# Two attention layers on one core: where the softmax division stands, and how the row maximum is formed

## The chip, the cores and the metric

The kernel runs on one core of a Trainium2 chip, as one program. The metric is the device time of one execution in microseconds (us); of the kernel before three executions were timed, with a median of 2111.77 us (2107.32 to 2115.55).

## The reference, cut to what matters

The input x has the shape (2, 512, 512): 2 batches, 512 tokens, width 512, all fp32. Four blocks follow each other, each as `x = x + LN(block(LN(x)))`:

```
L0 attention: 32 query heads, 8 key/value heads of 128, rotary, causal
    attn = softmax(q k^T / sqrt(128) with mask);  out = (attn v) Wo^T
L0 feed-forward: one linear layer with low-rank terms
L1 attention: 32 heads of 128, biases, rmsnorm on q and k, no mask
    attn = softmax(q k^T / sqrt(128));            out = (attn v + bv) Wo + bo
L1 feed-forward: silu(x w1) * (x w3), then w2, each with low-rank terms
```

The softmax of a row is exp(s - max) divided by the sum of the row. The change is about this division, and in layer 1 about the maximum and the factor 1/rms of q (`rq`), which is a factor of a row of the scores.

## The kernel before, in words

All products are made exact to fp32 by splitting each operand into a high and a low part of type fp32r (`hi + lo = x`) and adding three matmuls, hi hi + hi lo + lo hi (`mm3`). So every operand costs a cast to `hi` (ScalarE or VectorE) and a subtraction for `lo` (GpSimd or VectorE) before TensorE may use it.

A unit is two heads of one batch; there are 32 units in each attention layer, 64 heads a layer. For each head and each tile of 128 queries (`qt`, four of them):

- `l0_score` or `l1_score`: the scores in a PSUM bank (`ps_s`). In layer 0 one VectorE instruction adds the mask and takes the maximum. In layer 1 VectorE reduces the bank to the maximum (`m`), and a second, one element wide, multiplies it by `rq` (`mr`).
- `softmax_tail`: ScalarE makes P = exp(scale s + bias) from the bank, with the sum of the row (`rs`); VectorE takes the reciprocal (`ri`, one column); `nc.mul` multiplies the tile of P by it, on whichever of GpSimd, VectorE and ScalarE is done first by the program's own estimates. The page names this tile `ar`, as all large tiles.
- In most units (`lag`: units 2 to 26 of layer 0 and, counting on, 33 to 62, so 55 units or 110 heads) P is then transposed as 32 x 32 blocks on VectorE, written to DRAM (`pc` in layer 0, `pd` in layer 1), and read back with the blocks in place. Two tiles of queries make one such read of four DMAs. Casts and subtractions give `hi` and `lo` of P^T.
- `av_items`: O^T = V^T P^T in a PSUM bank (`ps_oy`), about one head later. ScalarE casts it to `hi`, VectorE subtracts for `lo` (the two `ot` tiles), in layer 1 with the bias `bv`.
- `out_proj`: y += O Wo, four matmul groups a unit.

In the other units (`pv_items`) P is transposed on TensorE at once.

The order of every engine's instructions is fixed when the program is built. A planner in the same file keeps a clock for TensorE and for each engine, with costs of its own; an item of TensorE's work is issued when its condition (`ok`) holds on that clock, and each stage of the other engines' work is issued at the time at which the planner expects its input. All DMAs are issued by SyncE, in one queue, in the planned order. The large tiles come from an arena of 37 slots of 4 KB a partition, each of which holds one full or two half tiles; `NBUF` and `PHASES` bound how many of each kind may live.

Of the kernel before, what the change touches and what calls it, by code (L numbers as in the profile page):

```python
# [19 lines left out]
S = 512  # L20
D = 512
P = 128
# [34 lines left out]
class Item:  # L57
    """a piece of TensorE's work, to be issued when cond holds"""
# [5 lines left out]
class Engine:  # L64
    """An engine that keeps its order of issue, with a clock (us) of its work."""
# [58 lines left out]
class Engines:  # L124
    WEIGHT = dict(vector=1.0, scalar=0.5, gpsimd=0.0)

    def pick(self, *cands):
        """issue the one of the candidates (engine, op, args...) that is done first"""
        def score(x):
            e = getattr(self, x[0])  # L130
            kw = x[-1] if isinstance(x[-1], dict) else {}
            c = e.cost(x[1], [y for y in x[2:] if not isinstance(y, dict)], kw)
            t = max(e.free, e.k.now + LAT)
            for y in x[2:]:
                if isinstance(y, bass.AP) and y.space == PSUM:
                    t = max(t, e.k.banks.get(y.name, 0.0))
            return t + c * (1 + self.WEIGHT[x[0]])
        x = min(cands, key=score)
        kw = x[-1] if isinstance(x[-1], dict) else {}
        return getattr(getattr(self, x[0]), x[1])(*[y for y in x[2:] if not isinstance(y, dict)], **kw)  # L140
# [9 lines left out]
    def mul(self, out, a, s):  # L150
        """by a factor of each row"""
        self.pick(("gpsimd", "tensor_scalar", out, a, s, 1.0, ALU.mult, ALU.mult),
                  ("vector", "tensor_scalar", out, a, s, None, ALU.mult),
                  ("scalar", "activation", out, a, AF.Copy, dict(scale=s)))

    def copy(self, out, a):
        """from PSUM"""
        self.pick(("scalar", "copy", out, a), ("vector", "tensor_copy", out, a))
# [8 lines left out]
class Kern:  # L167
    """Work is written as items: functions, or generators that yield the time
    (of TensorE's work) after which their next stage is to be issued."""

    NBUF = dict(TN=1, KT=2, W=14, Wk=4, raw=3, bb=2, bqk=1, nat=2, qk=10, v=4, P=7, x=8, xn=2, pt=5, T=4, PT=3, ot=6, tmp=2, A=5,
                v32=2, q32=4, k32=3, p32=1,
# [44 lines left out]
    # the large tiles: a half or the whole of a slot each (halves of one type only in a slot)  # L217
    HALF = dict(W=2, Wk=1, nat=2, v=2, PT=2, TN=2, KT=2, raw=1, bb=1, bqk=1, qk=1, P=1, x=1, A=1, T=1, xn=1, pt=1, ot=1,
# [77 lines left out]
    def phase(self, i):  # L296
        """what is tuned for each phase of the work"""
        for k, v in PHASES[i].items():
            if k in self.NBUF:
                self.NBUF[k] = v  # L300
            elif k in self.nc.WEIGHT:
                self.nc.WEIGHT[k] = v
            else:
                setattr(self, k, v)
# [20 lines left out]
    def wait(self, tag, n=1):  # L325
        """in a stage: until n slots are free, first come first served"""
        q = self.queues.setdefault(tag, [])
        ticket = object()
        q.append(ticket)
        while q[0] is not ticket or not self.has(tag, n):  # L330
            yield 0.1
        q.pop(0)

    def low(self, eng):
        """in a stage of low priority: until the engine has nothing issued to it"""
        e = getattr(self.nc, eng)
        while e.free > self.now + 0.01:
            yield e.free - self.now
# [6 lines left out]
    def streams(self, main, fills, bg):  # L345
        """Issue the streams of items, each in its order: a fill when its nominal place in
        main has come, or main waits; bg starts at its nominal place."""
# [30 lines left out]
    def pe(self, t):  # L378
        """t: at the full clock, which TensorE has after a busy tick only"""
        s = max(self.clk, self.now)  # L380
        while s >= self.tick:
            self.warm = self.cols >= 3060
            self.cols = 0
            self.tick += 10.24 / 3
        self.cols += t * 2400
        self.clk = self.now = s + (t if self.warm else 2 * t)
# [6 lines left out]
    def mm3(self, out, pairs, start=True, stop=True):  # L393
        """exact hi/lo products: hi hi + hi lo + lo hi"""
        n = len(pairs)
        for i, (lh, ll, rh, rl) in enumerate(pairs):
            self.mm(out, lh, rh, start and i == 0, False)
            self.mm(out, lh, rl, False, False)
            self.mm(out, ll, rh, False, stop and i == n - 1)
# [6 lines left out]
    def setup(self):  # L406
# [11 lines left out]
        self.pd = [self.dr.tile([P, 2, 4, 256], F32, name=f"pd{i}") for i in range(3)]  # L418
        self.kd = {n: [self.dr.tile([P, 4, 256], F32, name=f"kd{n}{i}") for i in range(2)] for n in "kq"}
# [9 lines left out]
    def consts(self):  # L429
# [5 lines left out]
        nc.vector.scalar_tensor_tensor(self.g, self.gqk[:, 0:1], SCALE, self.gqk[:, 1:2], ALU.mult, ALU.mult)  # L435
# [6 lines left out]
    def split(self, hi, lo, raw):  # L442
        """hi + lo = raw exactly"""
# [105 lines left out]
    def resid(self, b, tt, lvl):  # L549
        """x of level lvl + 1 = x + LN(y); returned short of a constant of each row"""  # L550
# [10 lines left out]
        if lvl == 3:  # L561
# [10 lines left out]
            nc.sync.dma_start(self.xsrc(b, tt, 4), x)  # L572
            self.rel(x)
# [6 lines left out]
        def store():  # L580
# [8 lines left out]
            nc.sync.dma_start(self.xsrc(b, tt, lvl + 1), xo)  # L589
            self.rel(xo)  # L590
# [3 lines left out]
    def boundary(self, b, tt, lvl):  # L594
        """from the finished y of level lvl on"""
# [21 lines left out]
    def out_proj(self, b, first, last, ot, w, badd, lvl):  # L617
        """y += O Wo over the heads of this unit"""
# [62 lines left out]
    def softmax_tail(self, st, j, qt, ps, bias, scale, w):  # L681
# [3 lines left out]
        rs = self.t("rs", [P, 1])  # L685
        nc.scalar.activation(pr[:, :w], ps[:, :w], AF.Exp, bias=bias, scale=scale, accum_out=rs)
        yield
        self.rel(bias, ps)
        ri = self.t("ri", [P, 1])
        nc.vector.reciprocal(ri, rs)  # L690
        yield
        nc.mul(pr[:, :w], pr[:, :w], ri)
        yield
        self.rel(rs, ri)
        if not st.get("lag"):
            st["p", j, qt] = pr
            return
        # P^T = 32 x 32 blocks transposed on VectorE, and the blocks put in place on their way through DRAM
# [60 lines left out]

    def unit_done(self, st):  # L760
        """after the last use of V"""
# [5 lines left out]
    def pv_items(self, st, j, voff, causal, bias):  # L767
        """transposes of P, then O^T = V^T P^T, split"""
# [70 lines left out]
    def av_items(self, st, j, voff, bias):  # L839
        """O^T = V^T P^T by halves of the queries, split"""  # L840
# [4 lines left out]
        def av(h, kc):  # L845
# [17 lines left out]
            if j == 1:  # L863
                self.unit_done(st)
            oh = self.t("ot", [P, S], F32R)
            ol = self.t("ot", [P, S], F32R)
            if bias is None:
                nc.scalar.copy(oh, po)
                yield
                nc.vector.tensor_tensor(ol, po, oh.bitcast(F32), ALU.subtract)  # L870
            else:
                nc.scalar.activation(oh, po, AF.Identity, bias=bias)
                yield
                nc.vector.scalar_tensor_tensor(ol, po, bias, oh.bitcast(F32), ALU.add, ALU.subtract)
            yield
            self.rel(po)
            st["ot"].append((oh, ol))

        def ok(h, kc):
            return (("hl", j, h, kc) in st and "v" in st["v"] and ((h, kc) != todo[0] or self.free("ps_oy"))  # L880
                    and ((h, kc) != todo[-1] or self.free("ot", 2)))
        return [Item(lambda h=h, kc=kc: ok(h, kc), lambda h=h, kc=kc: av(h, kc), 0, True) for h, kc in todo]

# [13 lines left out]
    def l0_zero(self):  # L897
        """the parts of pd0 that stay unused"""
# [135 lines left out]
    def l1_pre(self, hp, b, w, lag):  # L1034
# [62 lines left out]
        def flip(n):  # L1097
            """the transposes as 32 x 32 blocks on VectorE, put in place on their way through DRAM"""
# [70 lines left out]
    def l1_score(self, st, j):  # L1169
        def one(qt):  # L1170
# [6 lines left out]
            m = self.t("m", [P, 1])  # L1177
            nc.vector.tensor_reduce(m, ps, AX.X, ALU.max, negate=True)
            yield
# [3 lines left out]
            mr = self.t("mr", [P, 1])  # L1183
            nc.vector.tensor_tensor(mr, m, r, ALU.mult)
            yield
            self.rel(m)
            yield from self.softmax_tail(st, j, qt, ps, mr, r, S)
# [47 lines left out]
    def f1_init(self):  # L1235
        """rows 0:16, 32:48, 64:80 of the pieces: hi of a low-rank factor, lo in block k; others 0"""
# [151 lines left out]
    def f1_post(self, js, b, sts, last):  # L1388
        """y += g W2 over the chunks of units js"""
# [32 lines left out]
    def run(self, nu0=16, nu1=16, nf=6):  # L1422
        # at the ends of a layer's units some run batch by batch, each then with weights of its own
# [18 lines left out]
        def pre(n):  # L1442
            """early, mid items and state of unit n"""
# [47 lines left out]
        # weights start this many units before (early, mid, late parts)  # L1491
# [144 lines left out]
def _layout(i):  # L1636
    """Layouts of the arrays only: transposes and tilings."""
# [45 lines left out]
```

## Time and profile before

| what | value |
| --- | --- |
| median of three executions | 2111.77 us |
| lowest, highest | 2107.32, 2115.55 us |
| the profiled execution: its span | 2117.8 us |
| mean granted TensorE clock in it | 0.993 |
| instructions | 41211 |
| DMA traffic in it | 370.54 MB, mean 175 GB/s |
| ScalarE busy | 1337.7 us (63%) |
| GpSimd busy | 1446.3 us (68%) |

The page gives no other time for the profiled execution than its span; this span is 6.0 us (0.3%) over the median. A row of the page is read as: engine, operation, output<-inputs by tile names, shape, count; then busy time in all, mean time of one in ns, and the idle time of the engine in front of it with the instruction that ended it. Nearly all instructions have one line of code, since a helper issues them, so rows are told apart by tiles and shapes. The stages can be told by time: layer 0 attention runs to about 700 us, its feed-forward to about 770, layer 1 attention to about 1900, and the layer 1 feed-forward to the end.

### The profile page before, as it was taken

How to read it: one execution, taken by the hardware profiler on the slowest of the kernel's cores; microseconds unless marked ns; L12 is line 12 of the kernel's file. 1: busy time of each engine (PE TensorE's matmuls, PEld its weight loads, DVE VectorE, ACT ScalarE, POOL GpSimd, SP SyncE). 2: the span in 40 equal slices, each digit the busy share in tenths (PEclk: the TensorE clock that was granted, in tenths of full speed). 3: DMA queues.
4: the chain of work that ended last, by engine and by line, in shares of the span. 5: the costliest groups of instructions: out<-in, count | busy, mean ns of one | idle time of the engine just before them, and what ended most of it. 6: DMA issues, size and time to landing. Idle time of an engine off the chain costs nothing.

```text
span 2117.8 us, 41211 instructions
## 1 busy us (share of the span) xinstructions
PE 2056.7 (97%) x12605; PEld 1827.5 (86%) x12605; DVE 1801.4 (85%) x4210; ACT 1337.7 (63%) x3247; POOL 1446.3 (68%) x1786
## 2 busy tenths in 40 slices
PE   8999999999999999999999999999999999989998
PEld 7888888888888798889899999999999898977886
DVE  7998899899888889889889999899989988888534
ACT  5776677577766668776666666666667666664212
POOL 5686678688875567877677777777777776774212
PEclk9999999999999999999999999999999999999999
DMA  2476567577652235887877777777777787763021
GB/s 98 127 183 166 145 185 183 143 200 199 177 159 66 71 103 166 244 232 223 227 202 229 220 227 211 207 221 219 225 206 232 213 240 212 224 178 93 31 67 44
DMA packets 476566, 370.54 MB, mean 175 GB/s; under 512 B 117400, under 2 KB 424488, under 8 KB 476344
## 3 DMA queue, kind: packets, MB, share of 16 engines
q1 hardware_dynamic: 476344, 367.91, 60.9%
q8 instruction: 99, 1.62, 0.3%
q14 instruction: 123, 1.01, 0.2%
HBM read 232.12 MB, written 135.66 MB: 174 GB/s over the span
## 4 chain that ended last, share of the span: by engine, by line
PE 54%; DMA 12%; DVE 9%; SPq 3%; issue 2%; POOL 2%; ACT 2%; DVEq 0%; ACTq 0%; POOLq 0%
PE ps_pj L102 23%; PE ps_oy L102 19%; PE ps_s L102 10%; DVE ar L102 6%; SPq L102 3%; DMA pd<-ar 3%; DMA ar<-pd 2%; POOL ar L102 2%; DMA kdk<-ar 2%; ACT ar L102 2%; DMA ar<-kdq 2%; DMA kdq<-ar 2%; PE ps_tr L102 1%; DMA ar<-pc 1%; DVE m L102 1%
## 5 line engine op out<-in xcount | busy, mean ns | idle before, releaser
L102 POOL TENSOR_TENSOR ar<-ar,ar 128x256 fp32r<-128x256 f32 (+4 forms) x1223 | 1058.3, 887 | 456.6 <-ACT ar L102 333.6
L102 PE MATMUL ps_oy<-ar,ar 128*128 128x256 f32 (+2 forms) x4014 | 832.2, 342 | 28.7 <-DVE ar L102 14.0
L102 PEld LDWEIGHTS ps_oy<-ar,ar 128*128 128x128 f32 x4014 | 653.5, 190 | 133.1 <-DVE ar L102 22.5
L102 ACT CAST ar<-ar 128x256 fp32r<-128x256 f32 (+3 forms) x1166 | 531.5, 490 | 305.4 <-DMA ar<-pd 117.1
L102 PE MATMUL ps_pj<-ar,xh 128*128 128x256 f32 (+1 forms) x3392 | 635.2, 285 | 0.9 <-POOL ar L102 0.6
L102 PEld LDWEIGHTS ps_pj<-ar,xh 128*128 128x128 f32 x3392 | 536.0, 190 | 14.5 <-POOL ar L102 1.1
L102 PE MATMUL ps_pj<-ar,xl 128*128 128x256 f32 (+1 forms) x1696 | 482.9, 285 | 0.0
L102 DVE STREAM_TRANSPOSE ar<-ar 128x256 f32<-128x256 f32 (+3 forms) x688 | 347.9, 533 | 16.9 <-DMA pd<-ar 9.7
L102 DVE TENSOR_TENSOR ar<-ps_pj,ar 128x512 f32<-128x512 f32 (+2 forms) x448 | 305.4, 683 | 52.5 <-PE ps_pj L102 44.8
L102 PE MATMUL ps_s<-ar,ar 128*128 128x512 f32 (+2 forms) x1252 | 338.5, 376 | 8.6 <-DVE ar L102 4.7
L102 PEld LDWEIGHTS ps_pj<-ar,xl 128*128 128x128 f32 x1696 | 322.9, 190 | 2.1 <-DVE xl L102 0.7
L102 PE MATMUL ps_pj<-xh,ar 128*128 128x512 f32 x816 | 286.6, 399 | 0.7 <-ACT xh L102 0.7
L102 DVE TENSOR_TENSOR y<-ps_oy,y 128x512 f32<-128x512 f32 x272 | 184.8, 680 | 81.8 <-PE ps_oy L102 80.2
L102 PEld LDWEIGHTS ps_s<-ar,ar 128*128 128x128 f32 x1252 | 214.5, 189 | 44.0 <-DVE ar L102 12.6
L102 DVE TENSOR_TENSOR ar<-ar,ar 128x256 fp32r<-128x256 f32 (+5 forms) x328 | 207.9, 652 | 51.1 <-ACT ar L102 50.1
L102 ACT ACTIVATE ar<-ps_s,mr,rq 128x512 f32<-128x512 f32 x256 | 198.6, 777 | 46.7 <-DVE mr L102 36.9
L102 PEld LDWEIGHTS ps_pj<-xh,ar 128*128 128x128 f32 x816 | 154.0, 189 | 31.7 <-ACT xh L102 1.1
L102 DVE TENSOR_REDUCE m<-ps_s 128x1 f32<-128x512 f32 x256 | 170.9, 673 | 6.2 <-PE ps_s L102 5.0
L102 ACT ACTIVATE ar<-ar,ri 128x512 f32<-128x512 f32 (+3 forms) x245 | 149.6, 621 | 38.3 <-DVE ri L102 37.1
L102 POOL TENSOR_SCALAR ar<-ar,ri 128x512 f32<-128x512 f32 (+3 forms) x202 | 133.0, 661 | 54.3 <-DVE ri L102 48.9
L102 PE MATMUL ps_pj<-xl,ar 128*128 128x512 f32 (+1 forms) x408 | 161.2, 395 | 0.0
L102 ACT ACTIVATE ar<-ps_s,m 128x512 f32<-128x512 f32 (+3 forms) x256 | 133.8, 526 | 23.4 <-DVE m L102 14.8
(91 smaller groups left out, 2105.5 us busy)
## 6 DMA issues: line engine op xcount, KB each, us to landing
pd<-ar SPq DMA_DIRECT2D x240, 256.0 KB, 3.7
ar<-pd SPq DMA_DIRECT2D x480, 128.0 KB, 3.3
ar<-pc SPq DMA_DIRECT2D x200, 128.0 KB, 3.0
ar<-in_wq SPq DMA_DIRECT2D x86, 256.0 KB, 4.1
ar<-in_wo SPq DMA_DIRECT2D x86, 256.0 KB, 3.6
kdk<-ar SPq DMA_DIRECT2D x31, 512.0 KB, 4.8
ar<-kdk SPq DMA_DIRECT2D x124, 128.0 KB, 4.0
kdq<-ar SPq DMA_DIRECT2D x31, 512.0 KB, 5.1
```

The lines of the kernel that those rows point to most:

```text
L102: r = self.k.tc.keep_in_program_order(f(*args, **kw))
```

## The change

In the 55 units with `lag` P is no longer divided. The sums of a head's four tiles go into one tile `rs4` of four columns; when the fourth is there, `row_factors` takes one reciprocal of all four, writes it to DRAM (`rd`, 128 rows of 16 bytes) and reads it back into a half slot `R`, the same 512 values in all 128 partitions. When O^T is complete, one VectorE instruction multiplies the PSUM bank by R into a new half slot `ob`, with R read at a step of four elements; the casts and subtractions for `ot` then read `ob`, and the layer 0 subtraction may go to GpSimd. The last group of an O^T is planned only when R is planned to be there. In layer 1, in all units, one VectorE instruction multiplies the scores in place by `rq` and takes the minimum in the same pass; the sign is turned (`-SCALE`), so the minimum is minus the maximum, and the exponential has the constant scale -1. In two places the planner keeps a tile until its store has landed. The comments are taken out, which changes no instruction. The core of the diff:

```diff
     NBUF = dict(...
-                v32=2, q32=4, k32=3, p32=1,
+                R=2, ob=1, rs4=3, ri4=2, v32=2, q32=4, k32=3, p32=1,
...
+        self.rd = [self.dr.tile([P, NT], F32, name=f"rd{i}") for i in range(3)]
...
-        nc.vector.scalar_tensor_tensor(self.g, self.gqk[:, 0:1], SCALE, self.gqk[:, 1:2], ALU.mult, ALU.mult)
+        nc.vector.scalar_tensor_tensor(self.g, self.gqk[:, 0:1], -SCALE, self.gqk[:, 1:2], ALU.mult, ALU.mult)
...
             nc.sync.dma_start(self.xsrc(b, tt, lvl + 1), xo)
+            yield
             self.rel(xo)
...
-        rs = self.t("rs", [P, 1])
-        nc.scalar.activation(pr[:, :w], ps[:, :w], AF.Exp, bias=bias, scale=scale, accum_out=rs)
...
-        ri = self.t("ri", [P, 1])
-        nc.vector.reciprocal(ri, rs)
...
-        nc.mul(pr[:, :w], pr[:, :w], ri)
...
+        if st.get("lag"):
+
+            if ("rs", j) not in st:
+                st["rs", j] = [self.t("rs4", [P, NT]), 0]
+            rs = st["rs", j][0]
+            nc.scalar.activation(pr[:, :w], ps[:, :w], AF.Exp, bias=bias, scale=scale, accum_out=rs[:, qt:qt + 1])
+            yield
+            self.rel(bias, ps)
+            st["rs", j][1] += 1
+            if st["rs", j][1] == NT:
+                self.spawn(lambda: self.row_factors(st, j, rs))
...
+    def row_factors(self, st, j, rs):
+
+        nc = self.nc
+        ri = self.t("ri4", [P, NT])
+        nc.vector.reciprocal(ri, rs)
+        yield
+        self.rel(rs)
+        d = self.rd[st["slot", j]]
+        nc.sync.dma_start(d, ri)
+        yield
+        self.rel(ri)
+        yield from self.wait("R")
+        R = self.t("R", [P, S])
+        nc.sync.dma_start(R, d.rearrange("(o p) t -> o (p t)", o=1).broadcast_to([P, S]))
+        yield
+        st["R", j] = R
...
+            yield from self.wait("ob")
+            t = self.t("ob", [P, S])
+            R = st["R", j]
+            nc.vector.tensor_tensor(t.rearrange("m (t p) -> m t p", t=NT), po.rearrange("m (t p) -> m t p", t=NT),
+                                    R.rearrange("m (p t) -> m t p", t=NT), ALU.mult)
...
+            self.rel(po, R)
             if bias is None:
-                nc.scalar.copy(oh, po)
-                yield
-                nc.vector.tensor_tensor(ol, po, oh.bitcast(F32), ALU.subtract)
+                nc.scalar.copy(oh, t)
+                yield
+                nc.sub(ol, t, oh.bitcast(F32))
             else:
-                nc.scalar.activation(oh, po, AF.Identity, bias=bias)
-                yield
-                nc.vector.scalar_tensor_tensor(ol, po, bias, oh.bitcast(F32), ALU.add, ALU.subtract)
+                nc.scalar.activation(oh, t, AF.Identity, bias=bias)
+                yield
+                nc.vector.scalar_tensor_tensor(ol, t, bias, oh.bitcast(F32), ALU.add, ALU.subtract)
...
-                    and ((h, kc) != todo[-1] or self.free("ot", 2)))
+                    and ((h, kc) != todo[-1] or ("R", j) in st and self.free("ot", 2)))
...
-            m = self.t("m", [P, 1])
-            nc.vector.tensor_reduce(m, ps, AX.X, ALU.max, negate=True)
-            yield
             while "rq" not in st:
                 yield 0.3
             r = st["rq"][:, 2 * qt + j:2 * qt + j + 1]
-            mr = self.t("mr", [P, 1])
-            nc.vector.tensor_tensor(mr, m, r, ALU.mult)
-            yield
-            self.rel(m)
-            yield from self.softmax_tail(st, j, qt, ps, mr, r, S)
+            m = self.t("m", [P, 1])
+
+            nc.vector.tensor_scalar(ps, ps, r, 3.0e38, ALU.mult, ALU.min, accum_out=m)
+            yield
+            yield from self.softmax_tail(st, j, qt, ps, m, -1.0, S)
```

More of the change, by code (lines that the diff above doesn't have):

```diff
@@ L215, in t @@
         return x
-    HALF = dict(W=2, Wk=1, nat=2, v=2, PT=2, TN=2, KT=2, raw=1, bb=1, bqk=1, qk=1, P=1, x=1, A=1, T=1, xn=1, pt=1, ot=1,
+    HALF = dict(R=1, ob=1, W=2, Wk=1, nat=2, v=2, PT=2, TN=2, KT=2, raw=1, bb=1, bqk=1, qk=1, P=1, x=1, A=1, T=1, xn=1, pt=1, ot=1,
                 tmp=1)
@@ L684, in softmax_tail @@
         pr = self.t("P", [P, S])
-        rs = self.t("rs", [P, 1])
-        nc.scalar.activation(pr[:, :w], ps[:, :w], AF.Exp, bias=bias, scale=scale, accum_out=rs)
-        yield
-        self.rel(bias, ps)
-        ri = self.t("ri", [P, 1])
-        nc.vector.reciprocal(ri, rs)
-        yield
-        nc.mul(pr[:, :w], pr[:, :w], ri)
-        yield
-        self.rel(rs, ri)
-        if not st.get("lag"):
+        if st.get("lag"):
[8 more added lines that the diff above has]
+                self.spawn(lambda: self.row_factors(st, j, rs))
+        else:
+            rs = self.t("rs", [P, 1])
+            nc.scalar.activation(pr[:, :w], ps[:, :w], AF.Exp, bias=bias, scale=scale, accum_out=rs)
+            yield
+            self.rel(bias, ps)
+            ri = self.t("ri", [P, 1])
+            nc.vector.reciprocal(ri, rs)
+            yield
+            nc.mul(pr[:, :w], pr[:, :w], ri)
+            yield
+            self.rel(rs, ri)
             st["p", j, qt] = pr
@@ L758, in softmax_tail @@
         self.rel(pt)
+    def row_factors(self, st, j, rs):
+        nc = self.nc
+        ri = self.t("ri4", [P, NT])
+        nc.vector.reciprocal(ri, rs)
+        yield
[7 more added lines that the diff above has]
+        nc.sync.dma_start(R, d.rearrange("(o p) t -> o (p t)", o=1).broadcast_to([P, S]))
+        yield
+        st["R", j] = R
     def unit_done(self, st):
@@ L864, in av @@
                 self.unit_done(st)
+            yield from self.wait("ob")
[3 more added lines that the diff above has]
+                                    R.rearrange("m (p t) -> m t p", t=NT), ALU.mult)
             oh = self.t("ot", [P, S], F32R)
             ol = self.t("ot", [P, S], F32R)
+            yield
+            self.rel(po, R)
             if bias is None:
-                nc.scalar.copy(oh, po)
+                nc.scalar.copy(oh, t)
                 yield
-                nc.vector.tensor_tensor(ol, po, oh.bitcast(F32), ALU.subtract)
+                nc.sub(ol, t, oh.bitcast(F32))
             else:
-                nc.scalar.activation(oh, po, AF.Identity, bias=bias)
+                nc.scalar.activation(oh, t, AF.Identity, bias=bias)
                 yield
-                nc.vector.scalar_tensor_tensor(ol, po, bias, oh.bitcast(F32), ALU.add, ALU.subtract)
+                nc.vector.scalar_tensor_tensor(ol, t, bias, oh.bitcast(F32), ALU.add, ALU.subtract)
             yield
-            self.rel(po)
+            self.rel(t)
             st["ot"].append((oh, ol))
```

## The prediction

> **What bounds the kernel now.** I read the page's busy line first, then busy time by stage, then TensorE's waits, its order of time in a dense stretch, the rows of what is removed, and SyncE's waits.
>
> ```profile
> PE 2056.7 (97%) x12605; PEld 1827.5 (86%) x12605; DVE 1801.4 (85%) x4210; ACT 1337.7 (63%) x3247; POOL 1446.3 (68%) x1786
> ```
>
> TensorE leaves 2117.8 - 2056.7 = 61 us, VectorE is next at 85%. By stage (columns: time, PE, PEld, DVE, ACT, POOL busy, clock, DMA share, GB/s):
>
> ```profile
> 100.00:600.00 500.00, 494.59 (x2705) 431.77 (x2704) 444.86 (x1181) 342.91 (x989) 380.79 (x461) 1.00 0.66 176
> 800.00:1100.00 300.00, 288.52 (x1949) 262.05 (x1950) 265.22 (x583) 214.30 (x485) 226.78 (x275) 0.99 0.76 219
> 1100.00:1700.00 600.00, 595.26 (x4184) 552.45 (x4183) 547.03 (x1213) 390.61 (x901) 448.90 (x544) 1.00 0.76 219
> 1700.00:1900.00 200.00, 186.04 (x1216) 169.47 (x1214) 168.04 (x384) 132.24 (x294) 147.41 (x184) 0.96 0.76 217
> ```
>
> The units that the change touches lie in these four rows. TensorE idles 5.4, 11.5, 4.7 and 14.0 us there, 35.6 in all. The other 25.7 us (start, the turn between the layers, the last feed-forward) are out of its reach.
>
> Whether busy means at its pace, the timeline answers, because starts can be subtracted:
>
> ```profile
> 1299.66 0.85 PE L102 MATMUL ps_s<-ar,ar 128*128 128x512 f32 x3
> 1300.36 1.89 PE L102 MATMUL ps_oy<-ar,ar 128*128 128x256 f32 x9
> ...
> 1302.44 0.40 PE L102 MATMUL ps_pj<-ar,xh 128*128 128x256 f32 x2
> 1302.68 0.28 PE L102 MATMUL ps_pj<-ar,xl 128*128 128x256 f32 x1
> 1302.80 0.40 PE L102 MATMUL ps_pj<-ar,xh 128*128 128x256 f32 x2
> ```
>
> Three matmuls of 256 columns take 0.36 us from start to start, three of 512 take 0.70. A layer 1 unit has 192 of the first (q, k, v, O^T) and 48 of the second (scores, output): 64 x 0.36 + 16 x 0.70 = 34.2 us. The stage 1100 to 1700 does 4184 matmuls, 240 in 34.4 us. So at most 0.2 us of a unit can be won there.
>
> Here a rule of the Trainium skill speaks otherwise (Trainium Kernel Development and Optimization, Performance Expectations): matmul busy time is a bad measure of the distance to the roofline, LDWEIGHTS busy a good one. By it 14% of the span, 290 us, would be open, and less work elsewhere could bring much. The starts above decide for me: weight loads of 0.19 us stand beside matmuls that follow each other without a gap. I take 35.6 us of idle time, plus some clock (0.96 between 1700 and 1900: about 7 us).
>
> What TensorE waits for, over the whole span (us, times, longest):
>
> ```profile
> PE ps_oy L102 <- DVE ar L102: 14.0, 17, 2.2
> PE ps_oy L102 <- POOL ar L102: 8.5, 14, 1.5
> PE ps_oy L102 <- ACT ar L102: 5.6, 7, 1.6
> PE ps_s L102 <- DVE ar L102: 4.7, 15, 0.5
> ```
>
> These are hi and lo parts that come late from three loaded engines: the kind of wait that lighter engines shorten.
>
> **The change, part by part.** Counts are from the instruction orders of both programs, durations from these rows or rows of the same form (busy, mean ns):
>
> ```profile
> L102 DVE TENSOR_REDUCE m<-ps_s 128x1 f32<-128x512 f32 x256 | 170.9, 673 | 6.2 <-PE ps_s L102 5.0
> L102 DVE TENSOR_TENSOR mr<-m,rq 128x1 f32<-128x1 f32 x256 | 92.2, 365 | 0.0
> L102 DVE RECIPROCAL ri<-rs 128x1 f32<-128x1 f32 x512 | 70.9, 146 | 10.7 <-ACT ar L102 10.4
> L102 DVE DVE_READ_ACCUMULATOR2_ANT m<- 128x1 f32 x256 | 35.1, 137 | 0.0
> ```
>
> *VectorE.* 440 of 512 reciprocals go: 440 x 0.138 = -61 us; 110 of four columns come, at the same row +17. The 256 `mr` go: -92. The 256 reductions become multiply-and-minimum in PSUM. The nearest row is layer 0's mask-and-maximum: 0.70 us at 512 columns plus 0.137 to read the result out, 0.837 x 256 = 214 in place of 171, +43 (0 if nothing is read out). VectorE's share of the divisions goes: -40. The 110 multiplications by R cost 110 x 0.68 (128x512 with one PSUM operand: 682 ns) = +75. In layer 0 the 50 subtractions from PSUM go (50 x 0.68 = -34), 19 of that size from SBUF come (+15). Layer 1's 60 subtractions move from PSUM (731 ns) to SBUF (818): +5. Casts and other subtractions that the planner deals anew: +4. Sum -68, 1801 to 1733.
>
> *The stride.* R is read at a step of four floats, which no row here shows. The skill (SBUF — State Buffer, Door 1, the note on cachelines) says that an access which crosses to a new 16-byte line pays a penalty; every element of R does. By the row 0.68 us, by the rule, if the read halves, 1.36 (my estimate, twice the row): 110 x 0.68 = 75 us more, and VectorE would be back at 1808. I take the row; a gain below it has no ground, since a PSUM read alone already takes 0.67. Even the upper end only restores today's load.
>
> *ScalarE.* 206 fewer divisions of four widths (119 x 0.71 + 35 x 0.51 + 29 x 0.61 + 23 x 0.40 = -130), exponentials with a constant scale 686 instead of 776 ns, 256 x 0.09 = -23, and about +21 of casts that it takes over: -132. *GpSimd.* Divisions -113, the scaling of K -14, layer 0's subtractions 37 x 1.3 = +48, the rest -15: -94.
>
> *Latency.* A tile of P loses reciprocal, division and two hand-overs (0.15 + 0.7 + some 0.3 us) and in layer 1 `mr`; O^T gains one multiplication (0.68). What is late next on the P^T path is what was there before: the transposes (0.7), the write (3.7) and the read (3.3).
>
> *SyncE and DMA.* 220 issues at 0.44 us (four take 1.75) = 97 us of a queue that in 1200 to 1600 waits for 192 of 400 us:
>
> ```profile
> SPq L102 <- DMA pd<-ar: 86.9, 44, 4.2
> SPq L102 <- DVE ar L102: 33.2, 47, 2.2
> SPq L102 <- DVE r L102: 16.7, 13, 3.2
> SPq L102 <- DMA kdk<-ar: 16.2, 10, 2.4
> ```
>
> The read of R waits until `rd` has landed; behind it stand P^T reads and weights. A 128-piece transfer lands in 2.3 to 4.4 us here (`gqk`); in the new order one to eleven, mostly four or five, other DMAs (0.44 us each) stand between write and read, so the stop is between 0 and about 2.6 us, and I take 0.5. R lands 3.1 (a 256 KB broadcast, `bo`) to 6.2 us (`bk` in the dense stage) later: 5.4 to 10.6 us after the reciprocal. P^T of the same tile needs 0.7 + 3.7 + 3.3 and several casts and subtractions of 0.4 to 0.8, and O^T comes after that, so R hides. If it didn't, VectorE would stop at the multiplication, with the subtractions for q, k and P^T behind it, and TensorE behind those. R adds 110 x 0.26 = 29 MB to 370 (8%).
>
> *Wait added on VectorE:* the multiplication waits for TensorE's last O^T matmul where ScalarE's cast waited before (`ACT ar <- PE ps_oy`, 70 us in all, for 128 heads: 0.5 us a head). VectorE gets up to 60 us of such stops for the 68 us of work that it loses: no net slack lost. *The order of matmuls* hardly moves: averaged over a stretch of the dense layer 1 stage O^T groups stand within 0.4 us of their old place, around 700 to 850 us up to 5 us earlier. So the new half slots (at most three of 74) don't squeeze the arena. The retained store tiles and the sign cost nothing: they touch 32 tiles and one column.
>
> **Sum.** I let the lighter engines take away a third of the 35.6 us: -12. 8% more traffic and later landings cost where the chain runs over DMA and TensorE already idles (800 to 1100, 1700 to 1900: 25.5 us); I give 15% of that, +4. Net -8: 2117.8 to about 2110. The profiled span is 6.0 us over the median, so 2104.
>
> **Rivals.**
> - *Forecast: little moves (0.44).* 2104, own range 2101 to 2122; 0.5% (10.6 us) is about what a measurement of this kernel can tell from no change.
> - *The waits mostly go (0.36).* For it: all three engines that make TensorE wait get lighter, and `mr` (median 0.22 us, longest 2.45) stalls VectorE. If two thirds of 35.6 us and the clock's 7 go, less 3 for DMA: -25, 2087. Against it: DMA landings hold a share of these waits.
> - *SyncE's queue sets the pace (0.20).* In 1200 to 1600 (23 heads) 112 of the 192 us are landings, and 80, or 3.4 us a head, are waits for engines, its slack. New are 0.9 us of issue and the stop. From a stop of 2.5 us on, every microsecond is paid 60 times in layer 1. At a stop of 3 us: 0.5 x 60 = 30, 2134 from 2104. For it: landing up to 4.4 us, traffic up. Against it: the DMAs between.
> - *The division isn't cheaper at all:* the strided read costs 1.36 us. VectorE stays at 85%, only ScalarE and GpSimd gain: -3, 2109; part of the first case.
>
> Faster by over 0.5%: 0.36; within: 0.44; slower: 0.20. The range reaches into both other cases: 2082 to 2136.
>
> **What would show it.** Right: VectorE near 1733, ScalarE 1206, GpSimd 1352, TensorE's busy time unchanged in 1100 to 1700, fewer waits of `ps_oy` and `ps_s`; R's multiplication at 0.68 us; SyncE's wait for `rd` under 60 us in all. Wrong: multiplications of 1.3 us, waits for `rd` of 2 us and more, VectorE idle before R's multiplication, or a TensorE stage that starts later than before.

## The result, and the profile after

The changed kernel took 2238.8 us (median of 4 executions, 2232.6 to 2243.9) beside 2111.8 us for the kernel before in the same session: a ratio of 1.060 [1.058, 1.063]. It is slower by 6%, outside the forecast's 2082 to 2136 us. The profiled execution took 2243.9 us, its span is 2242.1 us and its mean granted TensorE clock 0.98.

First the busy line of the page after, then its busy time by stage (columns as before: time, PE, PEld, DVE, ACT, POOL busy, clock, DMA share, GB/s).

```profile
PE 2102.6 (94%) x12605; PEld 1850.2 (83%) x12605; DVE 1830.6 (82%) x3873; ACT 1233.0 (55%) x3085; POOL 1388.4 (62%) x1625
```

```profile
100.00:600.00 500.00, 476.84 (x2529) 407.14 (x2528) 449.71 (x991) 281.99 (x852) 365.78 (x401) 0.99 0.74 189
800.00:1100.00 300.00, 279.00 (x1856) 251.73 (x1855) 250.36 (x523) 185.06 (x429) 204.29 (x246) 0.98 0.75 211
1100.00:1700.00 600.00, 564.24 (x3818) 518.71 (x3818) 493.56 (x1000) 335.81 (x809) 381.24 (x437) 0.97 0.77 216
```

No engine has become a bound: every one but TensorE is below 83% of a longer span, ScalarE and GpSimd far below. TensorE did the same 12605 matmuls. Its busy time grew by 46 us while its clock fell from 0.993 to 0.98, and its idle time by 78 us (2242.1 - 2102.6 = 139.5, from 61.1). In the dense layer 1 stage it starts 3818 matmuls in 600 us where it started 4184, so a unit of 240 takes 37.7 us instead of 34.4. The matmul count in a fixed stretch is the plainest measure of pace on this page, since the busy share hides that a matmul can stretch.

What TensorE waits for now, and then what SyncE's queue waits for (us in total, times, longest):

```profile
PE ps_oy L102 <- POOL ar L102: 39.1, 43, 2.5
PE ps_oy L102 <- DVE ar L102: 31.2, 34, 4.1
PE ps_oy L102 <- ACT ar L102: 15.0, 21, 2.3
```

```profile
SPq L102 <- DVE ar L102: 365.8, 276, 32.0
SPq L102 <- DMA pd<-ar: 166.9, 84, 5.0
SPq L102 <- DMA rd<-ri: 106.4, 53, 5.4
```

The waits of the O^T and output matmuls (`ps_oy`) rose from 28 to 85 us, with GpSimd in front, which has less work than before. So the releaser is not overloaded; it got its own input late. GpSimd waited 512 us for ScalarE's casts (334 before, but 441 in a run below that leaves out the two transfers, so only part of the rise is theirs), and ScalarE in turn waited for reads that had not landed, in layer 0 above all for those of P^T (43.7 us before):

```profile
ACT ar L102 <- DMA ar<-pc: 121.2, 67, 7.3
```

SyncE stands 106 us in front of the landing of `rd`, a wait that did not exist before.

VectorE's rows, kept apart by form (busy, mean ns | idle before):

```profile
L102 DVE TENSOR_SCALAR_CACHE_REDUCE ps_s<-ps_s,rq 128x512 f32<-128x512 f32 x256 | 189.9, 744 | 14.4 <-PE ps_s L102 14.0
L102 DVE TENSOR_TENSOR ar<-ps_oy,ar 128x512 f32<-128x512 f32 x110 | 117.9, 1072 | 3.7 <-DMA pd<-ar 1.9 <-PE ps_oy L102 1.0 <-issue 0.5
L102 DVE TENSOR_TENSOR ar<-ar,ar 128x512 fp32r<-128x512 f32 x81 | 71.0, 882 | 36.0 <-ACT ar L102 35.8
L102 DVE SCALAR_TENSOR_TENSOR ar<-ar,bvc,ar 128x512 fp32r<-128x512 f32 x60 | 67.1, 1118 | 7.2 <-ACT ar L102 7.2
L102 DVE DVE_READ_ACCUMULATOR ps_s<-ps_s,rq 128x1 f32 x256 | 35.2, 138 | 0.0
```

The second row is the multiplication by R (1.07 us), the fourth the bias subtraction, which now reads SBUF twice (1.12 us; from PSUM it was 0.73). VectorE has 29 us more work than before, not 68 less.

### The profile page after: what moved, and what is told of

The parts are those of the page before. It is cut to its first block, busy times and chain, and to the rows that moved or that the text cites. A ratio compares the mean times of both kernels' runs of the same rounds, so it can differ in the third digit from the quotient of the medians.

```text
span 2242.1 us, 40901 instructions
## 1 busy us (share of the span) xinstructions
PE 2102.6 (94%) x12605; PEld 1850.2 (83%) x12605; DVE 1830.6 (82%) x3873; ACT 1233.0 (55%) x3085; POOL 1388.4 (62%) x1625
## 5 line engine op out<-in xcount | busy, mean ns | idle before, releaser
L102 POOL TENSOR_TENSOR ar<-ar,ar 128x256 fp32r<-128x256 f32 (+3 forms) x1248 | 1125.7, 926 | 649.3 <-ACT ar L102 511.6
L102 PE MATMUL ps_oy<-ar,ar 128*128 128x256 f32 (+2 forms) x4014 | 858.8, 346 | 86.1 <-POOL ar L102 39.1
L102 ACT CAST ar<-ar 128x256 fp32r<-128x256 f32 (+4 forms) x1261 | 578.1, 491 | 493.9 <-DMA ar<-pc 121.2
L102 ACT ACTIVATE ar<-ps_s,m 128x512 f32<-128x512 f32 (+3 forms) x512 | 309.3, 606 | 137.8 <-DVE ps_s L102 76.1
L102 PE MATMUL ps_s<-ar,ar 128*128 128x512 f32 (+2 forms) x1291 | 353.5, 383 | 19.1 <-ACT ar L102 8.4
L102 DVE TENSOR_TENSOR ar<-ar,ar 128x256 fp32r<-128x256 f32 (+7 forms) x359 | 250.3, 711 | 102.5 <-ACT ar L102 100.6
L102 DVE TENSOR_SCALAR_CACHE_REDUCE ps_s<-ps_s,rq 128x512 f32<-128x512 f32 x256 | 189.9, 744 | 14.4 <-PE ps_s L102 14.0
L102 DVE TENSOR_TENSOR ar<-ps_oy,ar 128x512 f32<-128x512 f32 (+1 forms) x124 | 127.4, 1027 | 3.7 <-DMA pd<-ar 1.9
L102 ACT ACTIVATE ar<-ar 128x512 f32<-128x512 f32 (+1 forms) x144 | 90.5, 628 | 71.6 <-DVE ar L102 61.4
L102 DVE CUSTOM_DVE_ANT_0 ps_s<-ps_s,ar 128x512 f32<-128x512 f32 (+3 forms) x256 | 121.8, 491 | 6.8 <-PE ps_s L102 6.8
```

The lines of the kernel that those rows point to most:

```text
L102: r = self.k.tc.keep_in_program_order(f(*args, **kw))
```

## The experiments

**Theories.** After the result I held that SyncE's stop at the landing of `rd` was the cause (106 us of waiting, in front of reads of P^T). The rivals were that the two transfers cost as traffic, with no stop needed, and that the computing part (multiplication, longer subtractions, fused maximum) costs the time. All ratios are to the kernel before, timed on the same chip, with 95% intervals. As a measure of pace I give with some runs the length of a 240-matmul unit in the stage 1100 to 1700 us, 600 x 240 / count.

**The parts, one at a time.** The fused maximum alone (with the turned sign that it needs), and the rows of P divided as before:

```diff
...
-            m = self.t("m", [P, 1])
-            nc.vector.tensor_reduce(m, ps, AX.X, ALU.max, negate=True)
...
-            nc.vector.tensor_tensor(mr, m, r, ALU.mult)
+            nc.vector.tensor_scalar(ps, ps, r, 3.0e38, ALU.mult, ALU.min, accum_out=m)
...
-            yield from self.softmax_tail(st, j, qt, ps, mr, r, S)
+            yield from self.softmax_tail(st, j, qt, ps, m, -1.0, S)
```

> Only layer 1's fused maximum is taken over; the division stays on the rows of P. Theory SyncE (the stop of the DMA queue at the landing of rd makes the slowdown): no rd here, so the time of before within 0.5%, VectorE about 38 us lighter. Theory VectorE (long new VectorE instructions make it): the fused maximum is no long one (0.88 us in place of 1.04), so within 0.5% too, or a little faster. Theory plan (any change of the costs that the planner sees upsets the order): 1% or more slower.

Measured: 1.006 [1.004, 1.008], with VectorE at 1769 us (32 less than before). The moved division alone is the changed kernel with that edit undone:

```diff
...
+            nc.vector.tensor_reduce(m, ps, AX.X, ALU.max, negate=True)
...
-            nc.vector.tensor_scalar(ps, ps, r, 3.0e38, ALU.mult, ALU.min, accum_out=m)
...
+            nc.vector.tensor_tensor(mr, m, r, ALU.mult)
```

> Only the division is moved; layer 1 keeps the reduction and the product mr. Theories SyncE and VectorE: nearly all of the slowdown, 5 to 7% over before, with SyncE waiting about 100 us for rd. Theory plan: it may be anything between 1 and 8%.

Measured: 1.067 [1.064, 1.070]; SyncE waited 59 us for `rd`. So the division part makes the loss. That it alone loses more than the whole change (1.060) says that the parts do not simply add: every edit of the computing also gives the planner another order.

**Is it the stop?** In the changed kernel R's read is held back in the plan, so that other transfers get between:

```diff
         self.rel(ri)
+        yield 1.5
         yield from self.wait("R")
```

> The changed kernel, with the read of R planned 1.5 us later, so that two to seventeen other DMAs stand between the write of rd and the read. Theory SyncE: the wait for rd falls from 106 us to below 40 and the time to at most 1.03 of before. Theory VectorE: the wait falls, but the time stays at 1.05 or more. Theory plan: not told apart.

Measured: 1.076 [1.073, 1.079]. The wait for `rd` fell from 106 to 36 us, and the time rose. As the only cause the stop falls; SyncE's wait for `pd` rose from 167 to 210 us instead. The edit also changes the order of the plan, so the 1.6% more is no price of the distance.

Then the two transfers alone, on the kernel before: the reciprocals of a head are collected in one tile, written to `rd`, read back as R, and the last group of O^T is planned only when R is planned to be there, but the rows are divided as before and no instruction reads R.

```diff
+            ri = st["ri", j][0][:, qt:qt + 1]
...
+        nc.sync.dma_start(d, ri)
...
+        nc.sync.dma_start(R, d.rearrange("(o p) t -> o (p t)", o=1).broadcast_to([P, S]))
...
-                    and ((h, kc) != todo[-1] or self.free("ot", 2)))
+                    and ((h, kc) != todo[-1] or ("R", j) in st and self.free("ot", 2)))
```

> The kernel before with its division on the rows of P, and in addition the write of rd, the read of R and its half slot, as in the changed kernel, but no multiplication by R. Theory SyncE: at least 1.03 of before, with SyncE waiting for rd as in the changed kernel. Theory VectorE: within 1% of before, since no VectorE instruction is added. If only the traffic counts, some 1%.

Measured: 1.081 [1.079, 1.084], more than the whole change. The unit takes 38.5 us (3741 matmuls). Whatever the computing part does, the transfers alone are enough.

**Which of the transfers, and what in them?** The next kernels are this one with single transfers taken out and booked on the planner's clock only (`ghost`), so that all four engines' instructions stand in exactly the same order; only SyncE's queue and the traffic differ. With both only booked:

```diff
+    def ghost(self, x):
...
+        k.hw = max(k.hw + (0.62 if ram else 0.475), k.now + 0.6)
+        k.dma = max(k.dma, k.hw + 0.6) + nbytes(x) / 0.36e6 * (2 if run < 512 else 1)
...
-        nc.sync.dma_start(d, ri)
+        self.ghost(d)
...
-        nc.sync.dma_start(R, d.rearrange("(o p) t -> o (p t)", o=1).broadcast_to([P, S]))
+        self.ghost(R)
```

> The run with the two DMAs but no multiplication (1.081 of before) again, with both DMAs of row_factors only booked on the planner's clock and not issued: the order of all engines' instructions is that of that run to the last one. Theory plan (the new order itself, with the half slot R held and the last O^T group waiting for R, is what costs): still 1.06 or more. Theory SyncE (the issues and the stop at rd): 1.01 or less. Theory traffic (29 MB of reads and 14,000 small writes delay the other DMAs): 1.01 or less.

Measured: 0.9965 [0.995, 0.998], 2100.6 us. The new order costs nothing and even wins a third of a per cent; the other kernels of this family are read against this one. With the write alone:

```diff
-        nc.sync.dma_start(R, d.rearrange("(o p) t -> o (p t)", o=1).broadcast_to([P, S]))
+        self.ghost(R)
```

> The same, with the write of rd issued and the read of R only booked; the order is the same. Theory plan: as the one with none, 1.06 or more. Theory SyncE: no stop at rd without the read, 0.44 us of issue a head remain: 1.00 to 1.02. If the 128 writes of 16 bytes are what is dear: 1.04 or more.

Measured: 1.024 [1.021, 1.028], so the write costs 2.8%: 59 us over 110 writes, 0.54 us each. That lies between the forecasts, so the parts of the write are taken apart below. With the read alone, from the bias `bo` so that nothing links it to a write:

```diff
-        nc.sync.dma_start(d, ri)
+        self.ghost(d)
...
-        nc.sync.dma_start(R, d.rearrange("(o p) t -> o (p t)", o=1).broadcast_to([P, S]))
+        nc.sync.dma_start(R, self.a["bo"].rearrange("(o d) -> o d", o=1).broadcast_to([P, S]))
```

> The same, with the read issued, but from the 512 values of an input (bo), so that nothing waits for a write, and the write of rd only booked; the order is the same. Theory plan: 1.06 or more. Theory SyncE: no stop, so 1.00 to 1.02. Theory traffic: the broadcast of 256 KB a head is what delays the others, 1.04 or more.

Measured: 1.019 [1.016, 1.021], so the read costs 2.2%, 0.42 us each, in the range forecast for SyncE's queue and below that for the traffic; the one-row read below decides against the queue. With both, but unlinked, the write of `rd` and the read of `bo`:

```diff
-        nc.sync.dma_start(R, d.rearrange("(o p) t -> o (p t)", o=1).broadcast_to([P, S]))
+        nc.sync.dma_start(R, self.a["bo"].rearrange("(o d) -> o d", o=1).broadcast_to([P, S]))
```

> The run with both DMAs (1.081 of before), in the same order of instructions, but the read takes the 512 values of an input (bo), so it doesn't wait for the write of rd. If the stop of SyncE at the landing of rd makes what the two single DMAs (1.024 and 1.019) leave open: about 1.045. If two DMAs together are simply dearer than the sum (traffic, issue): 1.07 or more.

Measured: 1.058 [1.054, 1.061], between the forecasts. The two together cost 6.1%, about 1.1 (give or take 0.6) more than their sum, and the link (wait for the landing of `rd`, then read it) 2.4% on top, 1.081 - 1.058.

Where it shows: DMA issues of the kernel with both only booked, then of the kernel with the write (KB each, median us from issue to landing).

```profile
pd<-ar SPq DMA_DIRECT2D x240, 256.0 KB, 3.4
kdq<-ar SPq DMA_DIRECT2D x31, 512.0 KB, 4.4
pc<-ar SPq DMA_DIRECT2D x50, 64.0 KB, 2.5
```

```profile
pd<-ar SPq DMA_DIRECT2D x240, 256.0 KB, 3.8
kdq<-ar SPq DMA_DIRECT2D x31, 512.0 KB, 6.0
pc<-ar SPq DMA_DIRECT2D x50, 64.0 KB, 3.2
rd<-ri SPq DMA_DIRECT2D x110, 2.0 KB, 4.1
```

A transfer of 2 KB takes 4.1 us to land, longer than one of 256 KB, and the other writes land 0.4 to 1.6 us later than without it. Three runs ask what in this write costs. From a constant tile, so that it waits for no reciprocal; only its first row, so that the issue remains; and another write of 128 pieces in its place, of 512 bytes instead of 16, from a constant tile into a DRAM tile of 64 KB:

```diff
-        nc.sync.dma_start(d, ri)
+        nc.sync.dma_start(d, self.neg8[:, :NT])
```

> The run with the write only (1.024), in the same order, but the write takes a constant tile, so SyncE doesn't wait for the reciprocal of the fourth tile before it. If the write costs because the queue stops at the reciprocal: 1.005 or less. If because of its issue and its 128 pieces of 16 bytes: 1.02.

Measured: 1.027 [1.023, 1.031]: as with the reciprocals, so the wait for them is free.

```diff
-        nc.sync.dma_start(d, ri)
+        self.tc.keep_in_program_order(self.tc.nc.sync.dma_start(d[:1, :], self.neg8[:1, :NT]))
+        self.ghost(d)
```

> As the write from a constant tile, but of one row of 16 bytes in place of 128. Beside that run it tells the pieces from the issue: if equal, the issue is the cost; if back at 0.997 (the order with no DMA issued), the pieces are.

Measured: 1.002 [1.001, 1.003]: the issue and one piece cost at most 0.55 of the 2.8% (the next run, with the same issue, costs less).

```diff
-        nc.sync.dma_start(d, ri)
+        self.tc.keep_in_program_order(self.tc.nc.sync.dma_start(self.rw[st["slot", j]], self.ident))
+        self.ghost(d)
```

> The run with only the write from a constant tile (128 pieces of 16 bytes, 1.027), in the same order, with 128 pieces of 512 bytes in place of those of 16, so 64 KB in place of 2. If short pieces are what is dear: 1.01 or less. If any write of 128 pieces to DRAM costs this: 1.027 to 1.035.

Measured: 0.9986 [0.9975, 0.9997]: as many pieces and 32 times the bytes cost a tenth of what the short pieces do (0.2%).

```profile
pd<-ar SPq DMA_DIRECT2D x240, 256.0 KB, 3.7
kdq<-ar SPq DMA_DIRECT2D x31, 512.0 KB, 4.7
pc<-ar SPq DMA_DIRECT2D x50, 64.0 KB, 2.6
```

With 512-byte pieces the landings are nearly back. So it is the 16-byte pieces of a write to DRAM, and not the number of pieces, the bytes in all, the issue or the wait. One thing changed together with the length: the short pieces of a head lie side by side in 2 KB of DRAM, the long ones fill 64 KB. No run writes short pieces far apart, so whether their shortness or their closeness is dear is not shown. On the side of the read, one row of 2 KB instead of 128; short pieces in a read; and 128 different rows instead of one row 128 times:

```diff
-        nc.sync.dma_start(R, d.rearrange("(o p) t -> o (p t)", o=1).broadcast_to([P, S]))
+        self.tc.keep_in_program_order(self.tc.nc.sync.dma_start(R[:1, :], self.a["bo"].rearrange("(o d) -> o d", o=1)))
+        self.ghost(R)
```

> The run with the read only (1.019), in the same order, but only one row of 2 KB is read in place of 128. If the 256 KB of traffic cost: 1.00 or less. If the issue in SyncE's queue costs: 1.015 to 1.02.

Measured: 0.996 [0.994, 0.997]: the issue of a read is free.

```diff
-        nc.sync.dma_start(R, d.rearrange("(o p) t -> o (p t)", o=1).broadcast_to([P, S]))
+        self.tc.keep_in_program_order(self.tc.nc.sync.dma_start(R[:, :NT], self.a["bo"].rearrange("(p t) -> p t", t=NT)))
+        self.ghost(R)
```

> The run with only a read, in the same order, but 128 pieces of 16 bytes from bo in place of 128 of 2 KB. If short pieces are dear in either direction: about 1.02. If only short writes to DRAM are: near 0.996, as with one piece.

Measured: 0.998 [0.997, 0.999]: 128 pieces of 16 bytes are nearly free in a read (0.16%).

```diff
-        nc.sync.dma_start(R, d.rearrange("(o p) t -> o (p t)", o=1).broadcast_to([P, S]))
+        nc.sync.dma_start(R, self.a["wo1"][0][:, 0, :])
```

> The run with only the read (1.019), in the same order, but the 128 pieces of 2 KB come from 128 different rows of Wo in place of one row. If reading one row 128 times makes the cost: 1.005 or less. If 256 KB a head do, wherever they come from: 1.015 to 1.025.

Measured: 1.016 [1.014, 1.019], within the error of the one-row read (1.019). The price of the read is its 256 KB, not that all partitions want the same row.

How this reaches TensorE is seen in the waits of the stage 1100 to 1700, of the kernel with both only booked and then of the kernel with both transfers:

```profile
DVE ar L102 <- DMA pd<-ar: 3.8, 3, 1.7
ACT ar L102 <- DMA ar<-kdq: 9.7, 9, 2.0
PE ps_oy L102 <- DVE ar L102: 0.2, 1, 0.2
```

```profile
DVE ar L102 <- DMA pd<-ar: 41.0, 23, 5.5
ACT ar L102 <- DMA ar<-kdq: 30.5, 9, 6.2
PE ps_oy L102 <- DVE ar L102: 22.1, 11, 4.3
```

VectorE's next transposes need tiles that the write of P^T (`pd`) still reads, and ScalarE's casts need the reads of q (`kdq`). Both engines take their instructions in the order of the program, so 5 us in front of one instruction delay every `hi` and `lo` behind it, and TensorE gets those late. The DMA share in this stage is 0.75 in both kernels, so the share does not tell them apart.

SyncE, whose queue stops where a read needs a landed `pd`, stops longer too (whole span, the same two kernels):

```profile
SPq L102 <- DMA pd<-ar: 159.9, 96, 5.0
```

```profile
SPq L102 <- DMA pd<-ar: 264.2, 125, 5.6
```

Its stops at all landings rise from 300 to 564 us, of which those for `rd` are only 67. How much of the loss goes through this queue and how much through the engines' own waits, no run separates.

**The computing part.** In the changed kernel's own order (the same on all four engines, but for the operand of the multiplication), both transfers are booked only, and the multiplication reads a constant tile loaded once. The factors are left out of the result.

```diff
-        nc.sync.dma_start(d, ri)
+        self.ghost(d)
...
+        self.ghost(R)
...
-                                    R.rearrange("m (p t) -> m t p", t=NT), ALU.mult)
+                                    self.Rc.rearrange("m (p t) -> m t p", t=NT), ALU.mult)
```

> The changed kernel in its own order of instructions, with both DMAs of row_factors only booked; the multiplication reads a constant tile (512 values of bo, loaded once), so the factors of the rows are left out of the result. It tells what the change would be worth if the factors came for nothing. If the DMAs are the whole cause: 0.98 to 1.00. If the longer VectorE instructions (1.07 us at a step of four, 1.12 us with two operands from SBUF) cost as well: 1.01 to 1.03.

Measured: 1.009 [1.006, 1.012]. So in the changed kernel the transfers cost 1.060 - 1.009 = 5.1%, 109 us or 1.0 us a head, and the rest of the change does not gain what was forecast; it loses 0.9%. Three runs ask why. The step of four taken away:

```diff
-                                    self.Rc.rearrange("m (p t) -> m t p", t=NT), ALU.mult)
+                                    self.Rc.rearrange("m (t p) -> m t p", t=NT), ALU.mult)
```

> The changed kernel without its two transfers, as the run before that measured 2138.1 us (1.0087), but the multiplication of O^T reads the constant tile in its own order instead of at a step of four elements; as there, the factors are left out of the result. Theory A (the step costs what is left of the change, 0.9%): the multiplication falls from 1.07 to about 0.7 us, 110 x 0.37 = 41 us less VectorE, and the time comes to 0.997 to 1.003 of before. Theory B (the rest is the fused maximum and the longer subtractions from SBUF): the multiplication is shorter, the time stays at 1.006 to 1.009.

The multiplication in the run with the step, and then in order:

```profile
L102 DVE TENSOR_TENSOR ar<-ps_oy,Rc 128x512 f32<-128x512 f32 x110 | 118.1, 1074 | 2.5 <-PE ps_oy L102 1.5 <-issue 0.9
```

```profile
L102 DVE TENSOR_TENSOR ar<-ps_oy,Rc 128x512 f32<-128x512 f32 x110 | 74.5, 678 | 2.9 <-PE ps_oy L102 1.7 <-issue 1.1
```

Measured: 1.0055 [1.004, 1.007], between the two forecasts. The step is worth 0.40 us an instruction, 44 us of VectorE, and about 0.3% of time, hardly more than the error. It is not the main part. The division part alone, without transfers, with layer 1's old reduction and small product, the same edit as in the second run above (the factors are again left out):

> The division part alone without its two transfers: layer 1 keeps the reduction to the maximum and the small product with the row factor; the multiplication of O^T reads a constant tile at a step of four, so the factors are left out of the result. Theory A (the 0.9% of the change without transfers comes from the fused maximum, which alone measured 1.006): 0.999 to 1.004. Theory B (it comes from the multiplication and the subtractions behind it): 1.006 to 1.012. With a strided multiplication of 1.07 us and subtractions of 1.06 us VectorE should be near 1800 us.

Measured: 1.007 [1.0055, 1.008]; the first theory there falls, the division part, in the order that the planner gives it, costs without its transfers too. And the fused maximum, the first edit above, on the kernel with both only booked:

> Division of the rows as before, the two transfers only booked on the planner's clock (that order alone measured 0.9965), and the maximum fused with the row factor. Theory A (the fused maximum costs by itself, some 0.6% as it did alone): about 1.002 to 1.004. Theory B (the 0.6% was the order that the planner happened to find with it): 0.994 to 0.999, and this would be the fastest version.

Measured: 1.003 [1.002, 1.004], 0.64% above its base (0.9965), as the 0.6% alone, though VectorE gets lighter by 10 us here and 32 there. Two other pairs of runs don't repeat it: without transfers the change with the fused maximum (1.009) and without it (1.007) agree within their error, and with transfers it is the faster one (1.060 against 1.067). In all four pairs the order of the instructions changes along with the maximum, so 0.6% is not shown to be its price. The booked-only kernel stays the fastest version that leaves nothing out: 2100.6 us, by order alone (with a dead one-row read it took 2098.3, which the intervals don't separate).

## Why the prediction was wrong

- **What bounds the kernel: right.** TensorE does, and what makes it wait are late `hi` and `lo` parts. The pace argument held too: the fastest version runs a unit in 600 x 240 / 4223 = 34.1 us, the 34.2 computed from the starts, and no run went below that.
- **The step that failed: "15% of that, +4" for the transfers.** It priced them as more of the same traffic, 8% of bytes on stretches that already idle. Measured they cost 109 us in the changed kernel. Three terms were wrong in it. The write was priced by its landing (taken from a read, `gqk`; at 3.9 us it came out as forecast) and its issue only; its 128 pieces of 16 bytes, 2 KB in all and invisible in a sum of bytes, cost 2.8% (the issue at most 0.55 of that). The read's bytes cost 2.2%, where all of the transfers were given 0.2%. And the cost was confined to 800 to 1100 and 1700 to 1900, because TensorE idles there; yet the stage 1100 to 1700 lost most, 34.4 to 37.7 us a unit. A stage with 5 us of idle time in 600 has nothing in which a stall could hide. "So R hides" was right, and did not help: VectorE idled 3.7 us in all in front of the 110 multiplications, none of it named as a wait for R. The cost fell on other transfers and on those who waited for them.
- **SyncE's stop at `rd`: wrong size, and not the main cause.** "I take 0.5" a head, under 60 us; it was 106 us, 1.0 a head. The rival built on it forecast the right direction, but 2134 us. Its mechanism, the link, measured 2.4 of 8.5% in the kernel before with both transfers, and lengthening the distance (1.5 us in the plan) did not help. The stops that grew most were those at other landings, which the rival counted but held fixed.
- **VectorE, "1801 to 1733": it went to 1831.** Of the 97 us, the multiplication is about 43 (1.07 us, nearer the middle of 0.68 and 1.36 than to the row that I took), the bias subtractions 18 (1.12 instead of 0.82), the subtractions of 128x512 from SBUF 9 (the row rose by 23.6 us where 15 was counted), those of 128x256 16 (4 was counted for these and the casts together), and the fused maximum 11 (744 + 138 ns). The Trainium skill's cacheline note (SBUF — State Buffer, Door 1) was right in direction where I let the row decide; no row there had a step. In time the step was worth about 0.3%, near its error.
- **ScalarE and GpSimd: right in direction.** 1233 for 1206, 1388 for 1352.
- **"The lighter engines take away a third of the 35.6 us": wrong in sign.** Without its transfers the change has ScalarE at 1233 us and GpSimd at 1389, and TensorE idles 2137.3 - 2058.8 = 78.5 us (61 before). Its waits for GpSimd rose (`ps_oy` 17.0 us, 8.5 before); those for ScalarE moved from `ps_oy` (1.3, 5.6 before) to `ps_s` (5.6, 1.3 before). An engine's total says little about when one part is ready.
- **What stays open.** Why the computing part loses 0.9%. The step and the fused maximum hold some of it, but the numbers are near the 0.35% that order alone moved in the booked-only kernel. Why two kernels with the fused maximum took 0.6% longer with less VectorE work was not found: one thing that changed, beside the order, is that its pass over the bank cannot start before `rq` is known, where the old reduction could; no run separates that. Why both transfers cost 8.5% in the one order and 5.1% in the changed kernel's was not tried either; there the other engines have more room, and there were more waits to hide in.
- **What would show it, as announced.** Of the four signs of being wrong two came: waits for `rd` of 2 us (106 us over 53, the longest 5.4), and a TensorE stage that starts later (layer 1's first maximum 28 us later). The other two did not: the multiplication took 1.07 us, not 1.3, and VectorE hardly idled before it. TensorE's busy time from 1100 to 1700, forecast unchanged, fell from 595 to 564 us, with 9% fewer matmuls in it.

The Trainium skill states a rule that spoke against the change and that the prediction did not weigh (DMA: Bandwidth & Descriptors, Specifications): below 512 bytes a piece, a transfer does not run at line rate, since the DMA reads, modifies and writes. The runs agree for writes, where 16-byte pieces cost 2.8% and 512-byte pieces 0.2%; for reads they show no such price, 16-byte pieces cost 0.16%. The rule gives no time for a short write, so it would not have put a number on this one, but it says that its 2 KB are not to be priced as bytes. No run here shows the read-modify-write itself.

## What to carry to other kernels

Price a transfer by the size of its pieces and by its direction, and not by its bytes alone: here the read cost by its 256 KB, but a write of a few bytes from each of 128 partitions to DRAM delayed other transfers more than one 32 times as large. In a stage where the bound engine runs without gaps and the DMA share is 0.75, an added transfer is not hidden just because its own landing is early; what counts is whom it delays, through buffers and in-order engines. And before giving lighter engines a share of the idle time, ask of each wait what its operand was itself waiting for.

## What the runs showed of the hardware

- A write of 128 pieces of 16 bytes to DRAM lands in 3.9 to 4.7 us and delays others (a 512 KB write from 4.4 to 6.0 us), though the trace gives each of its packets only 9 ns, 8 us of 16 engines for all 14080. Packet times and the DMA share do not show what it costs.
- A VectorE multiplication of 128x512 with one operand in PSUM takes 678 ns when the SBUF operand is read in order and 1074 at a step of four floats. The bias subtraction takes 1.01 to 1.12 us with both large operands in SBUF and 0.72 to 0.75 with one in PSUM.
- Stalls went with a slower clock. In one and the same order of instructions, with no transfer, the read, the write, both unlinked and both linked, TensorE idled 2, 17, 23, 40 and 46 us in the stage 1100 to 1700, and its granted clock there was 1.00, 0.99, 0.98, 0.97 and 0.97.
